# The norm's y on 128 partitions and two half pieces of 64

## The chip, the cores and the metric

The kernel runs on one core of one Trainium2 chip. The metric is the device time of one execution in microseconds (us). The engines are PE (TensorE, with PEld for its weight loads), DVE (VectorE), ACT (ScalarE), POOL (GpSimd) and SP (SyncE, here a queue of DMAs). Everything concerned here is float32.

## The reference, cut to what matters

The input is `x` of 4 images, 96 channels and 128 x 128 positions. A first layer makes 192 inner channels, runs a scan over four directions, and ends with a layer norm over the 192 channels of each position and a projection to 96:

```python
ym = (y0 + y1 + y2 + y3).reshape(B, D_INNER, H, W)
yn = jnp.moveaxis(ym, 1, -1)
mu = yn.mean(-1, keepdims=True)
var = yn.var(-1, keepdims=True)
yn = (yn - mu) * jax.lax.rsqrt(var + 1e-05) * ln_w + ln_b
yn = jnp.moveaxis(yn, -1, 1)
return jnp.einsum('bdhw,cd->bchw', yn, out_w) + out_b[None, :, None, None]
```

The result is added to `x`. A second layer then takes a group norm, splits the values by sign, computes an attention whose weights are convolution kernels, two further convolutions, and the output. The change concerns only the layer norm and its projection, called the norm here.

## The kernel before, in words

The scan (`ssm_scan`) leaves its sum over the four directions in the DRAM tensor `yms`, 192 channels by 16384 positions for each image. `ssm_output` is the norm of one image. It goes through 16 pieces of 1024 positions (`SN`), each of two halves of 512 (`CH`, one PSUM bank). A piece c passes these steps; three pieces are under way at once:

- `load_y` brings 192 channels as 96 partitions by 2 parts by 1024, one DMA on SP, three buffers. It is called for piece c + 1 in the fourth step of piece c.
- `squares(c, j)` squares part j on ACT.
- `sums(c, j)` multiplies y and its squares by a constant of 1/192 on PE (L960). The four products of a part go to four sets of 32 partitions of one bank: mean and mean square, for both halves. The two parts accumulate.
- `rows` copies that bank to SBUF on ACT (`st`, L972 and L974) and four small DMAs on ACT's queue turn it into 32 x 32 values (`mq`).
- `inverse`, `roots` and `back` make 1/sqrt(var + eps) on DVE and ACT; POOL's queue writes it to DRAM and `spread_out` reads it back onto 96 partitions (`r`), while SP loads `xr`, the piece of x.
- `projected(c, h)` is the projection of half h on PE (L1012), two products of 96 rows to 96 columns into one bank. Its weights `outws` have the norm's weight folded in and are centred over the 192 channels, so the mean need not be subtracted.
- `scaled(c, h)` multiplies the bank by r on DVE (L1025, or L1027 for image 0), `added` adds x on POOL, `counted` takes statistics on DVE, and SP stores the result.

Float32 products are two instructions each in the profile, so L1012 is 256 products and 512 instructions.

`co_run` alternates two generators by the costs that they yield. The norm of image 0 is emitted beside the scan, with three PSUM banks (`psl`). The norms of images 1, 2 and 3 are emitted beside other work, with two banks (`psr`): image 1 beside `direct_maps` of image 0, images 2 and 3 beside the attention. A bank is taken in turn by the first half's projection, the second half's projection and the sums. Up to the end of the scan `in_order` chains every engine's instructions in the order of emission; after it no such chain is set, and the framework orders them. In each round of six steps, with `old` = c - 2, the projection's halves stand apart:

```python
if old is not None:
    po = projected(old, 0)
...
yield 1.2
...
if old is not None:
    scaled(old, 0, po)
    po = projected(old, 1)
    ys.pop(old)
```

The second half is scaled in the third step, where `sums(c, 0)` stands too; `sums(c, 1)` is in the fourth and `rows(c)` in the fifth.

`other_weights` prepares the weights once, at the start, beside the projections of image 0. Loads of x for the statistics of images 1 and 2 go through POOL's queue then.

Of the kernel before, what the change touches and what calls it, by code (L numbers as in the profile page):

```python
# [9 lines left out]
F32 = mybir.dt.float32  # L10
BF16 = mybir.dt.bfloat16
AF = mybir.ActivationFunctionType
# [5 lines left out]
C = 96  # L18
H = W = 128
L = H * W  # L20
CH = 512
# [32 lines left out]
SN = 1024  # L54
# [17 lines left out]
def kernel(  # L72
# [26 lines left out]
    nc = tc.nc  # L99
    NB = x.shape[0]  # L100

    const = ctx.enter_context(tc.tile_pool(name="const", bufs=1))
# [51 lines left out]
    def filled(value, name, n=C, p=C):  # L154
        t = const.tile([p, n], F32, name=name, tag=name)
        nc.vector.memset(t, value)
        return t

    mean96 = filled(1.0 / C, "mean96")
    mean192 = filled(1.0 / (2 * C), "mean192", 32)  # L160
    zeros = filled(0.0, "zeros", 72)

    def clear(to):
# [61 lines left out]
    def other_weights():  # L225

        wdt = const.tile([128, 3, NK, 128], BF16, name="wdt", tag="wdt")
        wbc = const.tile([128, 3, 2, 128], BF16, name="wbc", tag="wbc")
        outws = const.tile([C, 2, C], F32, name="outws", tag="outws")
        outbs = const.tile([C, 1], F32, name="outbs", tag="outbs")
        with (
            tc.tile_pool(name="w0", bufs=1, side="right") as w0,
            tc.tile_pool(name="ps0", bufs=1, space=PSUM, side="right") as ps0,
        ):
            wf = w0.tile([RANK, NK, 2 * C], F32, name="wf")
            nc.gpsimd.dma_start(wf, dt_wT)  # L240
            outw = w0.tile([C, 2, C], F32, name="outw")
            nc.sync.dma_start(outw, out_wT)
            one = w0.tile([3, 128], BF16, name="one")
            nc.vector.memset(one, 1.0)
            nc.vector.memset(wdt, 0.0)
            nc.vector.memset(wbc, 0.0)
            yield
            flat = "p k c -> p (k c)"
            pieces = split3(w0, wf.rearrange(flat), [RANK, NK * 2 * C])
            for row, ch, g, p, n in (  # L250
                (row, *part)
                for img, *part in PARTS
                for row in ((KI * img,) if part[1] == 1 else (0, 64))
            ):
                for w in range(3):
                    yield
                    src = pieces[w].rearrange("p (k c) -> p k c", k=NK)[:, :, ch : ch + n]
                    for i in range(3):
                        at = row + w * 18 + i * RANK
                        nc.gpsimd.dma_start(wdt[at : at + RANK, g, :, p : p + n], src)  # L260
                for q in range(2):
                    at = row + 54 + q
                    nc.gpsimd.dma_start(wbc[at : at + 5 : 2, g, q, p : p + n], one[:, :n])
            for j in range(2):
                nc.vector.tensor_scalar(
                    outws[:, j], outw[:, j], lnw[:, j : j + 1], None, ALU.mult
                )
            pb = ps0.tile([C, 1], F32, name="pb")
            for j in range(2):
                nc.tensor.matmul(  # L270
                    pb, lhsT=outw[:, j], rhs=lnb[:, j : j + 1], start=(j == 0), stop=(j == 1)
                )
            nc.vector.tensor_add(outbs, pb, outb)

            mean = w0.tile([C, C], F32, name="mean")
            nc.vector.memset(mean, 1.0 / (2 * C))
            pw = ps0.tile([C, C], F32, name="pw")
            for j in range(2):
                nc.tensor.matmul(
                    pw, lhsT=mean, rhs=outws[:, j], start=(j == 0), stop=(j == 1)  # L280
                )
            nc.vector.tensor_sub(outws, outws, pw.unsqueeze(1).to_broadcast([C, 2, C]))
        yield wdt, wbc, outws, outbs

    def bank(ps):

# [2 lines left out]
    def part(ps, *shape):  # L289
        n = 1  # L290
        for d in shape[1:]:
            n *= d
        t = bank(ps)[: shape[0], :n]
        return t if len(shape) == 2 else t.rearrange("p (a b) -> p a b", b=shape[2])
# [636 lines left out]
    def ssm_output(b, yms, xnew, stats, ps, side, turned):  # L931
# [4 lines left out]

        with tc.tile_pool(name="c2", bufs=2, side=side) as p2:
            xb = x[b].rearrange("c h w -> c (h w)")
            ym = yms.rearrange("(j p) l -> p j l", j=2)
            rd = dram.tile([L], F32, name="rd")  # L940
            ys, sums_of, near, made = {}, {}, {}, {}

            def load_y(c):
                if c < NS:
                    ys[c] = p2.tile([C, 2, SN], F32, name="y", bufs=3)
                    nc.sync.dma_start(ys[c], ym[:, :, bass.ts(c, SN)])

            def squares(c, j):
                sq = p2.tile([C, SN], F32, name="sq")
                nc.scalar.activation(sq, ys[c][:, j], AF.Square)  # L950
                sums_of[c, j] = sq

            def sums(c, j):
                sq = sums_of.pop((c, j))
                if j == 0:
                    sums_of[c] = bank(ps)
                pm = sums_of[c]
                for g in range(4):
                    rhs = sq if g % 2 else ys[c][:, j]
                    nc.tensor.matmul(  # L960
                        pm[32 * g : 32 * g + 32],
                        lhsT=mean192[:, 0:32],
                        rhs=rhs[:, bass.ts(g // 2, CH)],
                        start=(j == 0),
                        stop=(j == 1),
                    )
# [39 lines left out]
                nc.gpsimd.dma_start(r, to.partition_broadcast(C))  # L1006
                near[c] = xr, r

            def projected(c, h):
                po = part(ps, C, CH)  # L1010
                for j in range(2):
                    nc.tensor.matmul(  # L1012
                        po,
                        lhsT=outws[:, j],
                        rhs=ys[c][:, j, bass.ts(h, CH)],
                        start=(j == 0),
                        stop=(j == 1),
                    )
                return po

            def scaled(c, h, po):
                r = near[c][1][:, bass.ts(h, CH)]
                if turned:
                    v = r.rearrange("p (h j t) -> p h j t", t=TN, j=TW)
                    nc.vector.tensor_mul(v, turned_view(po), v)  # L1025
                else:
                    nc.vector.tensor_mul(r, po, r)  # L1027
# [16 lines left out]
            for c in range(NS + 2):  # L1044
                new, old = c < NS, c - 2 if c >= 2 else None
                mid = c - 1 if 1 <= c <= NS else None
                if old is not None:
                    po = projected(old, 0)
                if mid is not None:
                    inverse(mid)  # L1050
                if new:
                    squares(c, 0)
                yield 1.2
                if mid is not None:
                    roots(mid)
                if old is not None:
                    scaled(old, 0, po)
                    po = projected(old, 1)
                    ys.pop(old)
                if new:  # L1060
                    squares(c, 1)
                yield 1.4
                if mid is not None:
                    back(mid)
                if old is not None:
                    added(old, 0)
                    scaled(old, 1, po)
                if new:
                    sums(c, 0)
                yield 1.4  # L1070
                if new:
                    sums(c, 1)
                if old is not None:
                    added(old, 1)
                    counted(old, 0)
                    load_y(c + 1)
                yield 1.4
                if new:
                    rows(c)
                if mid is not None:  # L1080
                    xr = near[mid][0]
                    nc.scalar.activation(xr, xr, AF.Identity, bias=outbs)
                    spread_out(mid)
                if old is not None:
                    counted(old, 1)
                yield 1.4
                if old is not None:
                    nc.sync.dma_start(xnew[:, bass.ts(old, SN)], near.pop(old)[turned])
                yield 1.4
# [1346 lines left out]
    class Image:  # L2436
# [50 lines left out]
    zb, yms = (  # L2487
        [dram.tile(shape, F32, name=f"{n}{p}", tag=f"{n}{p}", bufs=1) for p in range(npair)]
        for n, shape in (("zb", [2, 2 * C, NU, H, UW]), ("yms", [2, 2 * C, L]))
    )  # L2490
# [21 lines left out]
    with tc.tile_pool(name="wp", bufs=1, side="left") as wp:  # L2512
# [7 lines left out]
        for images, pace in (([0], 0.25), ([1], 0.75), ([2, 3], 1.35)):  # L2520
            left = projections(images, weights, stats, wp, psl)
            if images[0] == 0:
# [16 lines left out]
                wdt, wbc, outws, outbs = got  # L2539
# [148 lines left out]
```

## Time and profile before

| | |
|---|---|
| median of 3 runs | 6464.4 us (6441.7 to 6468.2) |
| the profiled execution | 6470.8 us, span 6468.9 us |
| PE busy | 5321.3 us, 82% of the span |
| DVE, ACT, POOL busy | 4711.2, 3786.8, 3238.6 us (73, 59, 50%) |
| granted PE clock, mean | 0.889 |
| projection L1012 | 512 instructions, 313.6 us busy |
| sums L960 on y, on the squares | 512 and 512 instructions, 215.8 and 164.7 us busy |
| squares L950 | 128 instructions of 1.04 us, 129.9 us |

The span runs from the first to the last instruction; the execution's own time includes what lies around it. A busy time is the union of a group's instructions, so products that lie side by side count once. Shares are averages over stages that are bound in different ways: the scan, the maps and the attention. What a waiting engine waited for is inferred from semaphores, and a wait for several is put down to the last. Line numbers are those of the kernel before.

### The profile page before, as it was taken

The page shows a single profiled execution, that of the slowest core. Times are in us where ns is not written, and L with a number is a line of the kernel's source. Part 1 is how long each engine was busy: PE and PEld are TensorE (multiplying, and loading weights), DVE is VectorE, ACT ScalarE, POOL GpSimd, SP SyncE. Part 2 cuts the span into 40 slices and gives each one's busy share as a digit, 9 for nine tenths or more (in the row PEclk, how much of TensorE's full clock was granted, in tenths as well). Part 3 has the DMA queues.
Part 4 walks back from the last instruction along what each step waited for, and adds up shares of the span by engine and source line. Part 5 has one row for each costly group of instructions (what it writes and reads, how often), then busy time and mean ns, then how long its engine had stood idle before and what let it go on. Part 6 is the DMA issues. An engine that isn't in the chain of part 4 may idle for free. (4 is left out here: it accounts for less than half of the span.)

```text
span 6468.9 us, 76257 instructions
## 1 busy us (share of the span) xinstructions
PE 5321.3 (82%) x23264; PEld 2301.3 (36%) x23264; DVE 4711.2 (73%) x7132; ACT 3786.8 (59%) x4770; POOL 3238.6 (50%) x2472
## 2 busy tenths in 40 slices
PE   6889988987888753989988588877888877989888
PEld 2333323322222111444433234345333445345553
DVE  4247778988989668988934785468874587888757
ACT  1247767776787676777632565466533665545642
POOL 1226757978889544979821344346213266022310
PEclk9999989998998665999999799888988988999989
DMA  6767777775675766675666776665766655966668
GB/s 154 176 157 193 191 202 196 218 213 163 199 198 163 214 173 215 197 217 174 199 182 185 187 220 161 164 157 155 213 195 164 178 145 155 243 174 181 191 170 219
DMA packets 891433, 1205.18 MB, mean 186 GB/s; under 512 B 228533, under 2 KB 743483, under 8 KB 878545
## 3 DMA queue, kind: packets, MB, share of 16 engines
q1 hardware_dynamic: 860496, 1145.35, 65.2%
q0 software_dynamic: 16208, 38.41, 2.2%
q10 hardware_dynamic: 14320, 16.54, 0.9%
q8 instruction: 187, 3.06, 0.2%
q14 instruction: 222, 1.81, 0.1%
HBM read 777.82 MB, written 345.62 MB: 174 GB/s over the span
## 5 line engine op out<-in xcount | busy, mean ns | idle before, releaser
L629 PE MATMUL bank<-y,wp 128*128 128x512 f32 (+3 forms) x3584 | 1320.2, 626 | 84.5 <-DMA y<-y 40.9
L862 POOL TENSOR_TENSOR y<-y,dl 128x1024 f32<-128x1024 f32 x384 | 1062.5, 2767 | 273.1 <-DVE dl L854 247.9
L829 POOL TENSOR_TENSOR dl<-dl,u 128x1024 f32<-128x1024 f32 x384 | 1015.8, 2645 | 247.1 <-ACT dA L805 129.5
L850 DVE TENSOR_TENSOR_SCAN dA<-dA,pBC 128x512 f32<-128x512 f32 x768 | 981.6, 1278 | 30.7
L1467 PE MATMUL two<-ya,wd 128*64 128x192 f32 (+3 forms) x2376 | 590.6, 422 | 201.7 <-ACT odd L1540 77.1
L629 PEld LDWEIGHTS bank<-y,wp 128*128 128x128 f32 (+3 forms) x3584 | 459.3, 169 | 755.8 <-issue 658.0
L854 DVE TENSOR_TENSOR dl<-dA,pBC 128x512 f32<-128x512 f32 x768 | 528.4, 688 | 260.0 <-PE pBC L743 187.1
L2159 PE MATMUL bank<-y,wn 128*64 128x384 f32 (+5 forms) x2408 | 665.2, 501 | 52.7 <-DMA y<-x1d 28.3
L743 PE MATMUL pBC<-xr,wbc 60*128 60x512 bf16 (+1 forms) x1536 | 458.5, 405 | 301.3 <-DVE dA L850 230.9
L1928 ACT COPY yb<-ya 64x768 f32<-64x768 f32 (+1 forms) x660 | 537.5, 814 | 202.6 <-PE two L1467 128.7
L672 ACT ACTIVATE dl<-pd,dtb 128x512 f32<-128x512 f32 x768 | 486.3, 684 | 183.2 <-PE pd L743 166.8
L1467 PE MATMUL two<-yb,wd 128*64 128x192 f32 (+3 forms) x2376 | 566.4, 407 | 4.0 <-ACT yb L1928 4.0
L833 DVE TENSOR_TENSOR pBC<-dl,pBC 128x512 f32<-128x512 f32 x768 | 527.5, 687 | 8.1 <-POOL dl L829 7.1
L2159 PEld LDWEIGHTS bank<-y,wn 128*64 128x64 f32 (+3 forms) x2408 | 306.9, 167 | 340.2 <-issue 150.9
L805 ACT ACTIVATE dA<-dl,negA 128x1024 f32<-128x1024 f32 x384 | 420.3, 1142 | 2.3
L1467 PEld LDWEIGHTS two<-ya,wd 128*64 128x64 f32 (+1 forms) x2376 | 266.9, 169 | 399.5 <-ACT odd L1540 87.8
L672 ACT ACT_TABLE_LOAD x248 | 318.2, 1283 | 94.9 <-PE pd L743 81.6
L743 PEld LDWEIGHTS <-wbc 60*128 60x128 bf16 (+1 forms) x1536 | 102.9, 96 | 749.3 <-issue 736.1
L1467 PEld LDWEIGHTS two<-yb,wd 128*64 128x64 f32 (+1 forms) x2376 | 295.1, 170 | 153.6 <-issue 41.5
L1012 PE MATMUL bank<-y,outws 96*96 96x512 f32 x512 | 313.6, 752 | 11.4 <-DVE r L1025 8.7
L1467 PE MATMUL two<-ya,wa 128*96 128x384 f32 (+1 forms) x528 | 229.9, 519 | 72.1 <-DMA ya<-vp 27.4
L1540 ACT COPY odd<-two 128x384 f32<-128x384 f32 (+5 forms) x176 | 116.0, 659 | 286.7 <-PE two L1482 177.2
(316 smaller groups left out, 9210.2 us busy)
## 6 DMA issues: line engine op xcount, KB each, us to landing
u<-zb SPq DMA_DIRECT2D x192, 1024.0 KB
yms<-y SPq DMA_DIRECT2D x96, 512.0 KB
y<-yms SPq DMA_DIRECT2D x64, 768.0 KB
xn<-xnew SPq DMA_DIRECT2D x128, 384.0 KB
ya<-vp SPq DMA_DIRECT2D x120, 336.0 KB
y<-y SPq DMA_DIRECT2D x128, 258.2 KB
zb<-z SPq DMA_DIRECT2D x64, 512.0 KB
ya<-x1p SPq DMA_DIRECT2D x90, 336.0 KB
```

The source lines that it names most:

```text
L629: nc.tensor.matmul(blocks(pz[p:e]), lhsT=ws[k][:, d, c : c + e - p], rhs=window(ys[k], at, d, n), start=(i == 0), stop=(i == len(terms) - 1),)
L672: nc.scalar.activation(dst, src, AF.Softplus, bias=bias)
L743: nc.tensor.matmul(p, lhsT=w[rows], rhs=xr[rows, at : at + CH], start=True, stop=True)
L805: nc.scalar.activation(live[m]["dA"], live[m]["dl"], AF.Exp, scale=negA[:, g % 3, k : k + 1])
L829: nc.gpsimd.tensor_mul(t, t, u_view(n))
L833: nc.vector.tensor_mul(p, live[n]["dl"][:, bass.ts(half, CH)], p)
L850: nc.vector.tensor_tensor_scan(h, h, p, init, ALU.mult, ALU.add)
L854: nc.vector.tensor_mul(live[n]["dl"][:, sl], live[n]["dA"][:, sl], live[n]["C", half])
L862: nc.gpsimd.tensor_add(v, v, t.rearrange("p (a b) -> p a b", b=W))
L1467: nc.tensor.matmul(of(to[p:e], r), lhsT=w[:, i, c : c + e - p], rhs=tiles(t[k][PAIR[i]][:, SLOT[i]], o, r), start=(k == 0), stop=False,)
L1928: nc.scalar.copy(yb[k][64 * h - 64 : 64 * h, :, :n], ya[k][0:64, :, h * TN : h * TN + n])
L2159: nc.tensor.matmul(pc[p:e, :n].rearrange("p (h w) -> p h w", w=W), lhsT=w[:, c : c + e - p], rhs=v[:, :, 0:W], start=(i == 0), stop=(i == ...
```

## The change

A piece of y now lies as 128 channels by 1024 positions (`y`), and the other 64 channels as two half pieces of 512 positions (`yr`), the first on partitions 0 to 63 and the second on 64 to 127. A piece takes three DMAs on SP instead of one. The squares follow that shape: 128 x 1024 and 128 x 512. The sums take four products of 128 rows and four of 64 rows, and the constant has 128 rows. The projection of a piece is emitted whole in the first step, into two banks: two products of 128 rows, then two of 64 rows, one on either half of the partitions. The weights are stacked in the same way by four DMAs on POOL's queue at the start, the 64-row part twice. The steps of the other functions stay where they are.

```diff
-    mean192 = filled(1.0 / (2 * C), "mean192", 32)
+    mean192 = filled(1.0 / (2 * C), "mean192", 32, 128)
...
-        yield wdt, wbc, outws, outbs
+            for p, e, i, c, j in (
+                (0, C, 0, 0, 0), (C, 128, 0, 0, 1), (0, 64, 1, 32, 1), (64, 128, 1, 32, 1)
+            ):
+                nc.gpsimd.dma_start(stack[p:e, i], outws[c : c + e - p, j])
+        yield wdt, wbc, stack, outbs
...
-                    ys[c] = p2.tile([C, 2, SN], F32, name="y", bufs=3)
-                    nc.sync.dma_start(ys[c], ym[:, :, bass.ts(c, SN)])
+                    y, rest = ys[c] = [
+                        p2.tile([128, n], F32, name=m, bufs=3) for m, n in (("y", SN), ("yr", CH))
+                    ]
+                    nc.sync.dma_start(y, yms[0:128, bass.ts(c, SN)])
+                    for h in range(2):
+                        nc.sync.dma_start(
+                            rest[64 * h : 64 * h + 64], yms[128:192, bass.ts(2 * c + h, CH)]
+                        )
...
-                sq = p2.tile([C, SN], F32, name="sq")
-                nc.scalar.activation(sq, ys[c][:, j], AF.Square)
+                sq = p2.tile([128, CH if j else SN], F32, name=f"sq{j}")
+                nc.scalar.activation(sq, ys[c][j], AF.Square)
...
-                    rhs = sq if g % 2 else ys[c][:, j]
+                    rhs = sq if g % 2 else ys[c][j]
+                    p = slice(64 * (g // 2), 64 * (g // 2) + 64) if j else slice(0, 128)
                     nc.tensor.matmul(
                         pm[32 * g : 32 * g + 32],
-                        lhsT=mean192[:, 0:32],
-                        rhs=rhs[:, bass.ts(g // 2, CH)],
+                        lhsT=mean192[p],
+                        rhs=rhs[p, :] if j else rhs[:, bass.ts(g // 2, CH)],
...
-            def projected(c, h):
-                po = part(ps, C, CH)
-                for j in range(2):
+            def projected(c):
+                po = [part(ps, C, CH) for _ in range(2)]
+                y, rest = ys.pop(c)
+                for h in range(2):
                     nc.tensor.matmul(
-                        po,
-                        lhsT=outws[:, j],
-                        rhs=ys[c][:, j, bass.ts(h, CH)],
-                        start=(j == 0),
-                        stop=(j == 1),
+                        po[h], lhsT=outws[:, 0], rhs=y[:, bass.ts(h, CH)], start=True, stop=False
+                    )
+                for h in range(2):
+                    p = slice(64 * h, 64 * h + 64)
+                    nc.tensor.matmul(
+                        po[h], lhsT=outws[p, 1], rhs=rest[p], start=False, stop=True
                     )
                 return po
...
                 if old is not None:
-                    po = projected(old, 0)
+                    po = projected(old)
...
                 if old is not None:
-                    scaled(old, 0, po)
-                    po = projected(old, 1)
-                    ys.pop(old)
+                    scaled(old, 0, po[0])
...
-                    scaled(old, 1, po)
+                    scaled(old, 1, po[1])
```

More of the change, by code (lines that the diff above doesn't have):

```diff
@@ L232, in other_weights @@
         wbc = const.tile([128, 3, 2, 128], BF16, name="wbc", tag="wbc")
-        outws = const.tile([C, 2, C], F32, name="outws", tag="outws")
+        stack = const.tile([128, 2, C], F32, name="outws", tag="outws")
         outbs = const.tile([C, 1], F32, name="outbs", tag="outbs")
@@ L240, in other_weights @@
             nc.gpsimd.dma_start(wf, dt_wT)
-            outw = w0.tile([C, 2, C], F32, name="outw")
+            outw, outws = (w0.tile([C, 2, C], F32, name=n) for n in ("outw", "centred"))
             nc.sync.dma_start(outw, out_wT)
@@ L938, in ssm_output @@
             xb = x[b].rearrange("c h w -> c (h w)")
-            ym = yms.rearrange("(j p) l -> p j l", j=2)
             rd = dram.tile([L], F32, name="rd")
```

## The prediction

> **What bounds the kernel now.** I read the page's first part, then the stretches of the four norms, then who waited for whom inside each, then the timeline of single pieces. A norm handles an image in 16 pieces of 1024 positions. By the starts of the copies `st<-bank` (one per piece) the norms run at 2105 to 2370 us (image 0, beside the scan), 3245 to 3525 (image 1, beside the direct maps), 3950 to 4225 and 4815 to 5090 (images 2 and 3, beside the attention). The table of these stretches:
>
> ```profile
> core 0: us, PE busy (x) PEld busy (x) DVE busy (x) ACT busy (x) POOL busy (x), PEclk, DMA share, GB/s
> 2105.00:2370.00 265.00, 193.19 (x498) 45.49 (x497) 176.22 (x243) 171.73 (x189) 143.92 (x103) 0.67 0.72 207
> 3245.00:3525.00 280.00, 241.61 (x876) 93.36 (x873) 108.77 (x236) 84.01 (x123) 63.09 (x62) 0.90 0.70 188
> 3950.00:4225.00 275.00, 245.34 (x1256) 109.70 (x1255) 115.16 (x256) 122.81 (x164) 93.72 (x124) 0.89 0.62 164
> 4815.00:5090.00 275.00, 239.79 (x1243) 104.99 (x1240) 116.33 (x258) 123.22 (x164) 99.74 (x133) 0.88 0.65 170
> ```
>
> In norms 1 to 3 PE is busy 86 to 89% and no other engine is over 45%: PE sets the pace, so PE time saved there can be span saved. In norm 0 PE is busy 73% at a clock of 0.67, DVE 66%, ACT 65%: no engine is full, and a ring of waits sets the pace. Waits of norm 1, then of norm 0, some lines of each:
>
> ```profile
> PE bank L960 <- DVE r L1025: 20.3, 9, 4.4
> ...
> PEld bank L1012 <- ACT st L972: 8.3, 8, 2.0
> ```
>
> ```profile
> PE bank L960 <- ACT sq L950: 43.1, 14, 7.1
> ...
> ACT sq L950 <- DMA y<-yms: 11.2, 5, 7.1
> ```
>
> In norm 1 the sums' product (L960) waits for the DVE product that empties the projection's bank (L1025): there are two banks. The same line is 8.3 us (3 times) in norm 2 and 7.3 (4) in norm 3. In norm 0 PE waits for the squares.
>
> **Prices on PE.** One clean piece of norm 3 on PE's timeline (each float32 product is two instructions):
>
> ```profile
> 4892.45 0.62 PE L960 MATMUL bank<-y,mean 96*32 96x512 f32 x1
> ...
> 4894.30 3.67 PE L1012 MATMUL bank<-y,outws 96*96 96x512 f32 x8
> 4897.81 0.81 PE L1467 MATMUL two<-ya,wd 128*128 128x384 f32 x2
> ```
>
> Sums take 1.85 us (4892.45 to 4894.30), eight products in four slots: products that go to four different sets of 32 output partitions start within 0.03 us of each other. The projection takes 3.51 us (to 4897.81), eight passes of about 0.43 us one after another[...].
>
> [...] The scan's two products of 60 rows at partitions 0 and 64 start together, and a stack of four products of 32 rows does too. [...]
>
> ```profile
> 1180.72 2.03 PE L531 MATMUL bank<-z,xpw 128*32 128x512 f32 x8
> 1182.69 0.61 PE L743 MATMUL pBC<-xr,wbc 120*128 120x512 bf16 x2
> ```
>
> These are four slots of two passes side by side, two slots in 128 rows by 32 columns and two in 64 by 32: 1.97 us against 4 x 0.43 = 1.72, so two changes of mode cost 0.25, about 0.12 each. [...]
>
> **The change part by part.**
> (1) Sums: four products for the 128 channels and four of 64 rows for the two half pieces. Four slots before and after; one more change of mode: +0.12 us a piece.
> (2) Projection: two products of 128 rows (four passes) and two of 64 rows on different row halves and banks, which can lie side by side (two slots): six slots for eight, -0.86 us, and a change of mode, +0.12. With (1): **-0.62 us of PE a piece**. Over the 48 pieces of norms 1 to 3 that is -30 us if all of it reached the span; if the pair never lies side by side it is +0.24 x 48 = +12.
> (3) What of it reaches the span. In 16 of the 42 pieces whose projection is followed by sums, PE then waits for DVE's r (35.9 us in all). There PE would only wait longer: gain 0. That leaves 32. The second half's first product needs the bank that ACT's copy of the sums frees (0.59 us). Before, it comes after two products of the first half (1.71 us), now after one (0.85). In about half of the pieces the projection starts as the sums end (in the quoted one, at 4894.30), the copy ends some 0.7 us later, and 0.1 us is left. The trace shows that the order after the scan isn't the emission order (at 4009.25 a first product of the projection stands before seven of the sums): where the bank is late, the first half's 64-row product goes ahead and the pair is broken, with no gain and 0.24 lost. I take 20 of the 32 as whole and the rest even: 20 x 0.62 = **-12 us**, ends -30 and +12.
> (4) Squares: 96x1024 twice (1042 ns each, `sq<-y`) becomes 128x1024 and 128x512. The trace has ACT's copy of 128x512 at 583 ns and the softplus of that shape at 684, so about 0.6: -0.44 us x 64 = -28 us of ACT. In norms 1 to 3 ACT is under half busy and PE waits for it there only 4 us: nothing. In norm 0 PE waited for squares 14 times; but where the scan's products stand between (2305.83 to 2307.65) the second square is hidden. I take 10 x 0.44 = **-4 us**, ends 0 and -7.
> (5) Norm 0's PE saves 16 x 0.62, more at half clock. Its three banks leave no bank wait. I cost it at nothing, hidden behind the wait for squares. Both halves' projection now stands ahead of the scan's L743 products, delaying those by up to two slots, 1.7 us at half clock. DVE had 4.8 us of waits on them there: 0 to +8 us, taken as 0 since B is spread a half step ahead.
> (6) Loads: one of 768 KB becomes 512 KB and two of 128 KB: 128 more issues on SP, 0.37 us each (L946's median): 47 us of SP. On SP the loads of the maps, of ya and of xr are queued behind; PE waits for any DMA in norms 1 to 3 by 2.9 us a norm at most. A load goes out about half a piece (7 us) ahead of its use: nothing; in norm 0, where ACT waited for y 11.2 us, the first square needs 512 KB only: 0 to -5. Against it, [...] SP shows waits for unrelated DMAs (27.3 us for `mq<-st` in norm 1): 0 to +10. Taken as 0. [...]
> (7) Start: four DMAs more on POOL for the stacked weights, 0.52 us each as its other issues: 2 us of POOL, which is under a third busy in the first 320 us. They wait for DVE's centring, and the statistics' loads of x are queued behind; PE's projections are the cover. Nothing, at most +2.
>
> **The sum** is -12 - 4 = -16 us. The profiled execution took 6470.8 us (span 6468.9); it would take 6455. The median of the runs is 6464.4, 6.4 lower, so I forecast **6448 us**, which is -0.25%.
>
> **The rivals.**
> A, the whole saving arrives: the pair is whole in all 48 pieces, and the pieces where PE waited gain too because the ring turns sooner: -30 us, norm 0 by (4) and (5) -7 to -12. About -40: 6424. For it: PE at 86 to 89%, and pairs elsewhere that lie side by side. Against it: 16 waits on r, and the bank.
> B, the sums wait for the emptied bank, slower. Before, 1.71 us of the second half's products stand between the end of the first half and the sums. Now both halves end together, and the sums need the first half's bank, which takes a DVE product of 0.68 us behind whatever DVE has queued, and r's landing. Queued behind the waiting sums is all of the attention's PE work. If the 26 pieces without this wait get one of 1.71 us[...], and no pair is whole: 26 x 1.71 = 44, and 12 for (2): +56, 6520. Against it: other PE work often stands between (4014.88 on, after a projection). It turns the sign when the mean new wait exceeds the mean gain, 0.3 us a piece.
> C, the pair isn't side by side and nothing else moves: +12, less 4 of ACT: 6472. The trace's pairs speak against it.
> D, the order after the scan is planned anew, and other lines than the norm's move either way, by some 20 us that nothing here prices.
>
> **How the numbers follow.** A measurement of this kernel can tell about 0.5% (32 us) from no change: faster is under 6432, slower over 6497. Forecast and its neighbourhood 0.38, A 0.27, B 0.24, C 0.11; D widens each. Faster by over 0.5%: A and a little of the forecast, 0.30. Slower: most of B, D on C, 0.27. Within: 0.43. The range goes from A with some of D, 6395, to most of B, 6510; the likeliest case's own range is 6430 to 6466.
>
> **What the new profile would show.** Right: the two 64-row passes of L1012's successor start within 0.03 us of each other in over half of the pieces of norms 1 to 3, and a clean piece takes 4.7 us instead of 5.36. `sq` gets a group of about 0.6 us. PE's waits on r grow by less than 15 us in these norms, those on st stay under 20. Wrong: the pairs start 0.4 us or more apart (C, or the broken order), sums wait for r in most pieces (B), or the time moves in stretches with no norm (D).

## The result, and the profile after

The kernel after took 6410.94 us (median; 6393.95 to 6425.22), the kernel before beside it 6462.57 (6441.66 to 6468.81): a ratio of 0.9923, interval 0.9911 to 0.9935, some 50 us less. The forecast was 16 us less. The profiled execution took 6409.7 us (span 6407.8), against 6470.8 (6468.9): these two lie 61 us apart. One profiled execution can lie up to 18 us from the median of its kernel's runs, so stages below are read from profiles and the worth of a change from medians.

**Where the time went.** A norm ends where DVE starts to combine its statistics (`mv<-xstats`). Those four points and the span's end, in us:

| | norm 0 | norm 1 | norm 2 | norm 3 | end |
|---|---|---|---|---|---|
| before | 2370.3 | 3533.0 | 4240.0 | 5095.3 | 6468.9 |
| after | 2359.9 | 3532.6 | 4211.0 | 5032.7 | 6407.8 |
| difference | -10.4 | -0.4 | -29.0 | -62.6 | -61.1 |

The 10 us at norm 0 are gone at norm 1's end. All of the gain arises between the end of norm 1 and the end of norm 3. The table of the norms' stretches in the kernel after (columns as in the prediction; the stretches are cut to the new length of each norm):

```profile
core 0: us, PE busy (x) PEld busy (x) DVE busy (x) ACT busy (x) POOL busy (x), PEclk, DMA share, GB/s
2100.00:2350.00 250.00, 164.39 (x490) 33.80 (x491) 164.40 (x227) 158.51 (x182) 131.33 (x96) 0.76 0.71 208
3245.00:3525.00 280.00, 239.54 (x887) 87.16 (x888) 109.05 (x236) 77.61 (x124) 62.71 (x62) 0.92 0.69 187
3960.00:4205.00 245.00, 222.19 (x1228) 92.30 (x1224) 113.49 (x253) 115.13 (x162) 93.82 (x123) 0.99 0.65 179
4785.00:5030.00 245.00, 220.62 (x1232) 91.54 (x1231) 113.36 (x251) 114.36 (x161) 99.31 (x131) 0.97 0.66 188
```

The column that moved is one the prediction gave no price to: PEclk, the granted clock of PE. It was 0.89 and 0.88 in norms 2 and 3, and is 0.99 and 0.97. PE's busy share hardly changed (91 and 90%, for 89 and 87%).

PE's waits that answer to those shown before, norm 1 first and then norm 0:

```profile
PE bank L970 <- DVE r L1037: 20.7, 6, 7.9
...
PEld bank L1023 <- ACT st L982: 10.5, 11, 1.6
```

```profile
PE bank L970 <- ACT sq L959: 54.2, 15, 7.5
...
ACT sq L959 <- DMA yr<-yms: 5.1, 1, 5.1
```

The sums' wait for r in norm 1 did not grow (20.3 before). Norm 0's wait for squares grew by 11 us although the squares are shorter: what PE saved there turned into waiting, and that norm kept its length (246.6 us before, 246.3 after, first sums to last projection). The clock rose there too, from 0.67 to 0.76, and bought nothing: PE's idle time within the norm went from 58 to 83 us.

**The pair.** One piece of norm 3 on PE's timeline:

```profile
4995.53 1.88 PE L1023 MATMUL bank<-y,outws 128*96 128x512 f32 x4
4997.34 1.10 PE L1028 MATMUL bank<-yr,outws 64*96 64x512 f32 x4
4998.38 0.90 PE L1770 MATMUL two<-ident,ring 96*90 96x96 f32 x8
```

Four passes of 128 rows, then four of 64 rows in the time of two: the projection takes 2.85 us (4995.53 to 4998.38), where it took 3.51. The two 64-row passes start within 0.01 us of each other. The pair is whole in 16 pieces of norm 0, 6 of norm 1, 8 of norm 2 and 12 of norm 3: 26 of 48 in norms 1 to 3. In the others the first half's 64-row product ran before the second half's 128-row one.

**The clock.** PE's clock records show only 1.0 and 0.5, and 139 of the 140 stretches at 0.5 in each of the two kernels are whole multiples of 3.41 us. Between a norm's first sums and its last projection:

| | length | at half clock | PE work lost by it | PE idle |
|---|---|---|---|---|
| norm 2, before | 267.1 | 61.4 | 27.8 | 29.5 |
| norm 2, after | 239.2 | 6.8 | 3.4 | 20.8 |
| norm 3, before | 265.2 | 68.3 | 30.0 | 34.7 |
| norm 3, after | 238.4 | 17.1 | 8.5 | 23.3 |

The third number is half of the half-clock time in which PE was busy. These two norms got 54.7 us shorter; lost work fell by 45.9 and idle time by 20.1, so about 11 us more of PE work, counted at the full clock, lies inside them, which must be work of other lines, since the norm's own became less. The half-clock time of the two norms came in 11 spells of 11.8 us on average before, and in 7 spells of 3.4 us after: the spells became fewer and, above all, shorter.

How such a loss arises is seen best in the kernel before. Its waits from 4044 to 4058 us, in norm 2 (us, times, longest):

```profile
DVE r L1025 <- DMA r<-rd: 7.0, 1, 7.0
ACT mq L992 <- DVE mq L988: 6.2, 1, 6.2
...
PE two L1467 <- ACT odd L1540: 5.8, 1, 5.8
```

DVE waits for r to come back from DRAM. Its part of the next piece's variance (L988) is queued behind, so ACT's square root (L992) waits; ACT's `odd` of the attention is queued behind that, and PE waits for `odd`. PE's timeline there, the number in brackets being the idle time before:

```profile
4050.32 0.90 PE L1760 MATMUL two<-ident,ring 96*90 96x96 f32 x8
4057.05 0.91 PE L1467 MATMUL two<-ya,wd 128*64 128x192 f32 x4 [5.82 <-ACT odd L1540]
...
4062.48 2.02 PE L1012 MATMUL bank<-y,outws 96*96 96x512 f32 x2
```

The last line is two passes in 2.02 us; two like them took 1.10 us at 4009.25, at the full clock. The same kernel cut into the stretches ahead of the gap, after it, and later:

```profile
4030.00:4051.00 21.00, 20.40 (x84) 7.67 (x82) 4.08 (x9) 6.97 (x10) 10.93 (x16) 1.00 0.57 146
4057.00:4079.00 22.00, 21.95 (x72) 7.89 (x74) 9.71 (x19) 8.26 (x11) 6.45 (x7) 0.50 0.19 51
4079.00:4100.00 21.00, 20.96 (x120) 10.33 (x117) 9.30 (x24) 8.15 (x12) 7.71 (x13) 0.99 0.53 137
```

PE counts as busy in all three. In the second it does half the work for 22 us: a gap of 5.8 us was followed by a loss of 11. The price, half of the time at half clock, shows in the passes too: those of the sums start 0.43 us apart at 4893.33, at the full clock, and 0.85 us apart at 4064.44. Why the clock stayed low for 22 us with PE busy is not shown.

### The profile page after: what moved, and what is told of

The parts are those of the page before. It is cut to its first block, busy times and chain, and to the rows that moved or that the text cites. A ratio compares the mean times of both kernels' runs of the same rounds, so it can differ in the third digit from the quotient of the medians.

```text
span 6407.8 us, 76468 instructions
## 1 busy us (share of the span) xinstructions
PE 5253.4 (82%) x23264; PEld 2254.8 (35%) x23264; DVE 4699.9 (73%) x7132; ACT 3759.4 (59%) x4770; POOL 3238.6 (51%) x2476
## 5 line engine op out<-in xcount | busy, mean ns | idle before, releaser
L2169 PE MATMUL bank<-y,wn 128*64 128x384 f32 (+5 forms) x2408 | 680.1, 507 | 58.3 <-DMA y<-x1d 34.1
L1406 POOL TENSOR_TENSOR pl<-x 96x256 f32<-96x256 f32 (+3 forms) x396 | 275.2, 710 | 0.0
```

The costliest lines, as they stand in the source:

```text
L2169: nc.tensor.matmul(pc[p:e, :n].rearrange("p (h w) -> p h w", w=W), lhsT=w[:, c : c + e - p], rhs=v[:, :, 0:W], start=(i == 0), stop=(i == ...
```

## The experiments

**Parts of the change one by one.** Four kernels in one comparison (before: 6456.98).

The move alone, on the kernel before:

```diff
-    po = projected(old, 0)
+    po = [projected(old, h) for h in range(2)]
+    ys.pop(old)
 ...
-    po = projected(old, 1)
```

> The kernel before, its y as 96 x 2, with one edit: the projections of both halves stand together in the first step, in two banks. Four theories on the gain of about 50 us. PAIR (the two 64-row products side by side save PE time): nothing here, within 10 us of before, since no pair exists. MOVE (the second half's projection ahead of the sums is what helps): 30 to 50 us under before. LAYOUT (the loads and squares on 128 partitions, and the order that the framework makes of them after the scan): within 10 us of before, since loads and squares are as before. CLOCK (PE's idle stretches of 3 us and more are gone in norms 2 and 3, so that it stays at full clock): says nothing of the cause, but the time follows the idle stretches: where five or so of them stay in norm 2, the granted clock there stays at 0.88.

6456.49 us, ratio 0.9993 (0.9981 to 1.0006). The move by itself is worth nothing that can be measured. It keeps the low clock in norm 3:

```profile
4815.00:5090.00 275.00, 239.62 (x1245) 105.38 (x1245) 113.94 (x253) 122.13 (x164) 101.55 (x132) 0.88 0.64 169
```

The new layout with the halves projected in their old steps, so without a pair:

```diff
-def projected(c):
-    po = [part(ps, C, CH) for _ in range(2)]
+def projected(c, h):
+    po = part(ps, C, CH)
```

> The changed kernel with the projections put back: each half has its own bank, a 128-row product and then its 64-row product, first half in the first step, second half in the second step. Loads, squares, sums and weights as changed. PAIR: no gain, 0 to 15 us over before for the changes of PE's mode. MOVE: no gain. LAYOUT: 30 to 50 us under before. CLOCK: where it is fast, norms 2 and 3 show a granted clock over 0.95; where slow, about 0.88.

6434.91 us, ratio 0.9958 (0.9940 to 0.9977).

The kernel after with the four products half by half, again without a pair:

```diff
 for h in range(2):
     nc.tensor.matmul(po[h], lhsT=outws[:, 0], ...)
-for h in range(2):
     p = slice(64 * h, 64 * h + 64)
     nc.tensor.matmul(po[h], lhsT=outws[p, 1], ...)
```

> The changed kernel with the four products of a projection emitted half by half: 128-row and 64-row product of the first half, then of the second. Both halves still stand in the first step. No pair lies side by side, so PE has 0.86 us more a piece where the pair was whole (26 of 48 pieces in norms 1 to 3) and a change of mode more. PAIR: the gain is gone, within 10 us of before. MOVE: 25 to 45 us under before. LAYOUT: 25 to 45 us under before. By the direct price alone it is 26 x 1.1 = 29 us over the changed kernel at most.

6431.07 us, ratio 0.9962 (0.9949 to 0.9976). In neither is any pair side by side, and yet some 25 us are gained; the other 25 come with the pair, if the kernel after's 0.9923, from another comparison, is set beside these ratios. The group of the 64-row products in this kernel, then in the kernel after (busy us, mean ns of one, idle before):

```profile
L1027 PE MATMUL bank<-yr,outws 64*96 64x512 f32 x256 | 148.6, 662 | 0.0
```

```profile
L1028 PE MATMUL bank<-yr,outws 64*96 64x512 f32 x256 | 96.2, 637 | 0.0
```

The pair takes 52 us off the busy time of these products, norm 0's pieces included, where the norm gets no shorter by it. The 26 whole pairs of norms 1 to 3 save two slots of 0.43 us each: 22 us, which fits the measured 25. The layout's part shows in the clock of norms 2 and 3, here of the kernel half by half:

```profile
3960.00:4205.00 245.00, 228.10 (x1234) 93.56 (x1234) 113.45 (x251) 114.97 (x161) 95.84 (x124) 1.00 0.66 182
4803.00:5055.00 252.00, 232.38 (x1179) 91.71 (x1186) 112.42 (x244) 109.65 (x155) 98.12 (x130) 0.93 0.63 175
```

The kernel before with y loaded by parts, so two DMAs for one:

```diff
-nc.sync.dma_start(ys[c], ym[:, :, bass.ts(c, SN)])
+for j in range(2):
+    nc.sync.dma_start(ys[c][:, j], ym[:, j, bass.ts(c, SN)])
```

> The kernel before with one edit: the load of a piece of y is two DMAs, one for each part of 96 channels, instead of one. PE, ACT and DVE do the same work. PAIR and MOVE: within 10 us of before. LAYOUT by the loads (the first square needs only its own part): 5 to 20 us under before. If the order that the framework makes after the scan is what moves the time, this edit, which moves that order as far on PE as the change does, can come out anywhere within 30 us of before, on either side.

6445.56 us, ratio 0.9989 (0.9975 to 1.0003): 7 us less (from 16 less to 2 more), not told from nothing.

**The square, from both sides.** First the kernel after with its second square stretched back to the old length:

```diff
-nc.scalar.activation(sq, ys[c][j], AF.Square)
+nc.scalar.activation(sq.rearrange("p (a n) -> p a n", a=2),
+    ys[c][1].unsqueeze(1).to_broadcast([128, 2, CH]), AF.Square)   # j == 1
```

> The kernel after, with the second square of every piece stretched back to 128x1024 (the 512 columns are squared twice, the second copy is not used), so ACT pays about 1.04 us again instead of 0.6. Loads, sums and projection stay as in the kernel after. Theory S (the layout's gain in norms 2 and 3 comes from the shorter square, because it lets sqrt and with it r come earlier): half-clock time in norms 2 and 3 goes back over 35 us each, waits of DVE on r<-rd over 20 us, and about 20 to 26 us of the gain goes: 6430 to 6437 us. Theory L (it comes from the load of y by parts, or from the order of the work): time stays within 10 us of the kernel after, 6405 to 6420, with half-clock time below 25 us in both norms. In norm 0 both expect +0 to +5.

6430.74 us, ratio 0.9950 (0.9933 to 0.9968). The two kernels below that repeat the kernel after in the same comparison have 0.9911 and 0.9919, so the stretch costs 20 to 25 us. Some 3 us of that are pairs by estimate (4 times 0.86): 22 of 48 are whole here, for 26. The edit did what it says, by the group of the second square:

```profile
L960 ACT ACTIVATE sq<-yr 128x1024 f32<-128x1024 f32 x64 | 67.0, 1047 | 12.9 <-issue 6.2 <-DMA yr<-yms 4.9 <-DMA y<-x2d 1.6
```

But it took the time by another way than theory S said. Norms 2 and 3 kept their high clock:

```profile
3970.00:4215.00 245.00, 224.62 (x1215) 91.66 (x1214) 112.48 (x252) 119.64 (x160) 92.21 (x121) 0.98 0.65 177
4798.00:5043.00 245.00, 224.56 (x1209) 89.77 (x1208) 111.13 (x242) 119.11 (x159) 97.73 (x128) 0.97 0.66 184
```

Half-clock time is 10.2 and 13.7 us there, where theory S wanted over 35. One profile, whose stages scatter by some 10 us from kernel to kernel, does not show where the 20 us went.

Then the kernel before with the second square halved:

```diff
-nc.scalar.activation(sq, ys[c][:, j], AF.Square)
+n = CH if j else SN
+nc.scalar.activation(sq[:, 0:n], ys[c][:, j, 0:n], AF.Square)
 ...
-rhs=rhs[:, bass.ts(g // 2, CH)],
+rhs=rhs[:, bass.ts(0 if j and g == 3 else g // 2, CH)],
```

> The kernel before, with the second square of every piece cut to 96x512 (about 0.6 us for 1.04); the sums take the first half's squares of that part for the second half too, so the variance of the second half's positions is left wrong: part of the squares is left out. Loads, layout, number of products, projection as before. Theory S (ACT's shorter square is most of what the new layout brings, as stretching it back in the kernel after took about 20 us of the gain away): 6440 to 6450, about -20 us. Theory C (the square is worth nothing by itself; what stretching it back cost is part of the spread between kernels): within 8 us of the kernel before. Where it falls on S, the half-clock time of norms 2 and 3 tells whether it comes by the clock (under 35 us each, for 61 and 68) or not.

6434.82 us, ratio 0.9964 (0.9948 to 0.9980): 23 us (13 to 34) by less work for ACT alone, at the old layout. Here the clock does go along, in norm 2 more than in norm 3:

```profile
3961.00:4201.00 240.00, 217.80 (x1216) 101.17 (x1214) 110.28 (x251) 114.81 (x162) 94.33 (x123) 0.96 0.70 185
4793.00:5050.00 257.00, 227.79 (x1205) 100.60 (x1204) 110.36 (x242) 113.63 (x161) 97.44 (x128) 0.91 0.67 176
```

Half-clock time 20.5 and 47.8 us, for 61.4 and 68.3. So the shorter square is worth some 20 us whether it is put in or taken out, and theory C, that it is worth nothing, has fallen. How it brings them differs between the two kernels. And the square did not change alone: in their profiles 102 and 116 of the 4770 places in ACT's order hold another instruction than in the unedited kernels. The split load changed 185 such places for 7 us, which speaks against the order as the cause, but does not exclude it.

**Six kernels that missed their aim.** They were to make r come earlier or later in norms 1 to 3. Their edits take `turned` for true in image 0; it is true in images 1 to 3. So against what the texts on record say **they reached image 0 alone**. On PE, DVE and ACT the order of instructions stayed that of the unedited kernel.

```diff
+                if mid is not None and not turned:      # one step earlier (or later)
+                    spread_out(mid)
...
-                    spread_out(mid)
+                    if turned:
+                        spread_out(mid)
```

> The kernel before with one edit: for images 1 to 3 the read-back of r from DRAM is emitted one step (1.4 us of yielded cost) earlier, with the second part's sums instead of with the copy of the sums. No engine does less work. Clock theory (long waits of PE on the chain of r cost twice, once idle and once at half clock after it): the waits of DVE on r<-rd fall from 24-30 us a norm to under 15, gaps of PE over 3 us fall from 5 to 0-2 a norm, half-clock time in norms 2 and 3 from 61 and 68 us to under 30 each, and the time falls by 25 to 50 us: 6415 to 6440. Rival (the gain of the change is PE's shorter passes and the half clock only goes along with them): waits move to other lines and the time stays within 10 us of the kernel before. Third possibility (POOL's queue then holds its additions behind r's wait for the DRAM write): slower by 10 to 30 us.

> The kernel after with the same edit: r read back one step earlier for images 1 to 3. Clock theory: few long gaps are left in norms 2 and 3 (7 and 17 us of half clock), but norm 1 still has 44 us at half clock and five gaps over 3 us; it gains up to 20 us there if something else does not hold norm 1: 6390 to 6410. Rival: no change within 10 us. POOL held behind the wait: slower by 10 to 30 us.

> The kernel after with the opposite edit: for images 1 to 3 r is read back one step later, after the copy of the sums. No engine does more work. Clock theory: DVE's waits on r<-rd rise from 10-12 us a norm to over 20, gaps over 3 us come back in norms 2 and 3 (3 or more each) and with them 35 us or more at half clock in each, and the time rises by 25 to 50 us: 6435 to 6460. Rival (the half clock is not tied to r's lateness, the gain is the shorter passes): the time stays within 10 us of the kernel after.

The early read gave 0.9992 (0.9977 to 1.0007) on the kernel before and 0.9911 (0.9889 to 0.9932) on the kernel after; the late one on the kernel after gave 0.9919 (0.9898 to 0.9941). None differs measurably from its unedited kernel. They decide nothing on the clock theory.

```diff
-nc.gpsimd.dma_start(r, to.partition_broadcast(C))
+(nc.gpsimd if turned else nc.sync).dma_start(r, to.partition_broadcast(C))
```

> The kernel before with r read back on SP's queue instead of POOL's for images 1 to 3; the order on PE, DVE and ACT is unchanged. On POOL the read stands behind additions and waits, 7 to 9 us after the write's issue, which lands after 3 to 4. Clock theory: r lands up to 3 us earlier where POOL held it, DVE's waits on r fall under 18 us a norm, half-clock time in norms 2 and 3 from 61 and 68 us to under 40, time -15 to -40. Rival 1 (the wait is not POOL's doing, the chain in front of the write is late): within 10 us. Rival 2 (SP's loads of ya, the maps and xr stand behind the wait for the write): slower by 10 to 40 us.

> The kernel after with the same edit, as a candidate that may beat it: norm 1 still has 44 us at half clock and DVE waits for r of 11 to 18 us a norm. If r comes earlier without holding SP: -5 to -20 us, 6390 to 6405. If SP is held: +10 to +40. Else within 8 us.

1.0012 (1.0000 to 1.0023) and 0.9934 (0.9917 to 0.9950): reading image 0's r on SP's queue brings nothing. No kernel tried is measurably better than the kernel after.

For norms 1 to 3 these kernels, and the next one, are repeats. Half-clock time in norms 2 and 3 together was 130, 126 and 89 us in the kernel before and its two repeats, and 24, 34, 44, 48 and 38 in the kernel after and its four. It scatters, but the two groups do not meet: the difference in clock belongs to the kernels, not to one execution.

```diff
+rd2 = rd if turned else dram.tile([L], F32, name="rd2")
 ...
 nc.gpsimd.dma_start(to.rearrange("(p f) -> p f", f=TN), q)
+if not turned:
+    again = rd2[bass.ts(c, SN)]
+    nc.gpsimd.dma_start(again, to)
+    to = again
```

> The kernel after with r's way lengthened for images 1 to 3: POOL copies each piece's 1024 values from one DRAM tensor to another before r is read back, one more DMA of 4 KB, some 4 us from issue to landing as rd's own, POOL waiting for the first to land. The order of all work on PE, DVE and ACT is that of the kernel after, so only the lateness of r changes. Clock theory (each long gap of PE is paid again at half clock): DVE's waits on r<-rd rise from 11 to 18 us a norm to over 30, gaps of PE over 3 us from 0-1 to 4 or more in norms 2 and 3, half-clock time there from 7 and 17 us to over 40 each, and the time rises by 40 to 90 us, of which a third or more is half clock. Rival (r has slack, or PE has other work to put there): within 12 us of the kernel after.

6440.57 us, ratio 0.9968 (0.9954 to 0.9981), 30 us more than the kernel after. By the profile all of it is norm 0: 279.6 us long for 246.3, while norms 2 and 3 took 241.6 and 242.0. Waits in norm 0, and one of them in the kernel after:

```profile
DVE xstats L1056 <- POOL xr L1052: 87.7, 23, 7.1
POOL rd L1009 <- DVE mq L1007: 71.9, 15, 8.2
...
POOL rd L1012 <- DMA rd<-mq: 53.7, 15, 6.3
```

```profile
DVE xstats L1051 <- POOL xr L1047: 27.7, 18, 1.8
```

POOL stands 3.6 us a piece until the first write has landed, so its additions come later, and DVE's statistics wait for these three times as long. Norm 0 gets 2.1 us a piece longer, which reaches the end. So norm 0 is sensitive to a hold on POOL's queue, found by accident: one link of the ring that the prediction spoke of. That the way of r sets norm 0's pace without the added copy is not shown: to read r earlier, later or on SP's queue in this same norm brought nothing. Nor did the shorter square and the pair, which both act there.

**All kernels side by side.** Half-clock time and PE's idle time are those of norms 2 and 3 together; the last column is the time from the end of norm 1 to the end of norm 3. All in us, from one profile each.

| kernel | ratio | half clock | idle | norm 1 to 3 |
|---|---|---|---|---|
| before | 1 | 129.7 | 64.2 | 1562 |
| before, image 0's r early; on SP | 0.9992; 1.0012 | 126.3; 88.7 | 66.6; 59.7 | 1558; 1541 |
| move alone | 0.9993 | 105.8 | 61.7 | 1545 |
| loads alone | 0.9989 | 109.3 | 36.1 | 1542 |
| short square alone | 0.9964 | 68.3 | 50.3 | 1519 |
| layout, halves apart | 0.9958 | 17.0 | 32.8 | 1512 |
| layout, half by half | 0.9962 | 34.1 | 36.4 | 1523 |
| after, long square | 0.9950 | 23.9 | 40.8 | 1507 |
| after | 0.9923 | 23.9 | 44.1 | 1500 |
| after, image 0's r early; late | 0.9911; 0.9919 | 34.1; 44.4 | 44.8; 48.9 | 1500; 1513 |
| after, image 0's r on SP; with the hop | 0.9934; 0.9968 | 47.7; 37.6 | 47.7; 44.3 | 1519; 1497 |

The last column follows the half-clock column from group to group: the kernel before and its two repeats have 115 us at half clock and 1554 us in the last column on average, the kernel after and its four have 38 and 1506. These 48 us match the measured 50. Every kernel with y on 128 partitions has little half clock. What ended PE's gaps of over 2 us in norms 2 and 3 tells which waits vanish. The sums' wait for r stays: 12.6 us on average over four kernels with y on 96 partitions (before, the move, and the two with only image 0's r changed), 14.9 over the five that keep the layout and order of after. The waits of the attention's products (`two`) for ACT's `odd` and `kt` and for DVE's `sm` fall from 32.7 us to 8.1. Between these two groups, the idle time that went was the attention's, not the norm's own.

But fewer waits alone do not bring the clock. With the loads alone split, these waits of the attention are 11.1 us and PE's idle time is 36.1, about as low as after, and yet there are 109.3 us at half clock and no gain that can be told. What sets the layouts apart is how long a spell lasts. After gaps of 2 to 3 us in norms 1 to 3, half clock followed about as often in the six kernels with y on 96 partitions (20 of 36 gaps) as in the eight with y on 128 (32 of 64), but in the median it lasted 10.0 us in the first and 3.8 us in the second.

**What stays open** is why. After the scan the framework orders the instructions anew for every kernel. To hold that order fixed while the layout changes was not tried. So whether the attention's waits went because ACT and DVE come to them sooner, or because their place in the queues changed, is not settled. Nor is it known what ends a half-clock spell, and so why spells are shorter with y on 128 partitions.

## Why the prediction was right or wrong

The forecast's range held the result and its likeliest case did not: it said 16 us, and the measured 50 lie outside its own range of 6430 to 6466. The better case, faster by over 0.5%, had 0.30. That the range held it is in part luck: its low end was put together from A and some of D, and the worth of the shorter square and the granted clock, which the runs point to, are in neither.

- **(1) and (2), prices on PE: right.** The projection takes 2.85 us, and 3.51 - 0.86 + 0.12 is 2.77; the sums with their mode change take 1.98 (3982.02 to 3984.00, norm 2) for 1.85 + 0.12. The starts side by side that these prices rest on measure, in the kernel before, under 0.01 us apart for the scan's two products of 60 rows (2200.24) and within 0.02 us for a stack of four of 32 rows (4326.02 to 4326.04).
- **(3), what reaches the span: mis-sized.** The reading of the bank and of the broken order was right in that a 64-row product ran ahead (in 22 of 48 pieces; that the bank was late in each of them was not shown), and 20 whole pairs were close to 26. But it charged the extra changes of mode, 0.12 us each by its estimate, to the span, and took the gain in the pieces with a wait as 0. Kernels that have these changes of mode and no pair are 25 us faster than before, not slower; the pair adds about 25, near the 22 that 26 whole ones bring at their full 0.86. The step took 12 us for what measured about 25.
- **(4), squares: the failed step.** Its duration was right (619 ns for "about 0.6") and so was the total (ACT's busy time 3786.8 to 3759.4, -27). Its worth was not: 4 us, and "in norms 1 to 3 ACT is under half busy and PE waits for it there only 4 us: nothing". Put in or taken out, it is worth some 20 us. PE waited little for the squares themselves; it waited for `odd` and `kt`, which stand in ACT's one queue with them, by 31.7 us in norms 2 and 3 of the kernel before. That this is the way of the 20 us is argued, not shown: with the long square put back the clock stayed high. And norm 0, where the 4 us were booked, gained nothing.
- **(5) norm 0 and (7) the start: right** within the scatter of single profiles, no gain and no loss. PE's saving went into a longer wait for the squares, as the step said.
- **(6), loads: right within the measurement**, 0.9989 for the split alone.
- **What no step priced is the granted clock.** PEclk of 0.89 and 0.88 stood in the very lines that the prediction quoted, and it read them as a busy PE. Of that busy time, 58 us in norms 2 and 3 were lost to the half clock.
- **The rivals.** B fell: the sums' waits for r were 20.7, 9.8 and 9.0 us in norms 1 to 3, against 20.3, 8.3 and 7.3. C fell, the pair lies side by side. A came nearest in size (40 us) but not by its mechanism: 22 of the 48 pairs are broken, norm 0 gave nothing, and half of the gain needs no pair. D was named without a price; of the 61 us between the two profiles 54.7 lie in norms 2 and 3, so its sign, time moving where there is no norm, did not appear, though a new order inside them may be part of the layout's gain.

## What to carry to other kernels

Read the granted clock of a stage beside its busy share before you call an engine the bound: a PE at 88% busy and a clock of 0.88 has lost time hidden in its busy time. In norms 2 and 3 of the kernel before PE was idle for 64 us and lost 58 more to the half clock, so the waits may cost about twice what the list of waits says. A saving on an engine that is far from full is not free of worth (here some 20 us came with 28 us less work for ACT), so look at who is queued behind it before costing it at nothing. And test that an edit reaches the images it names: a condition read the wrong way round cost six of these runs their question.

## What the hardware showed that was not expected

**Gaps and the clock.** PE's clock fell after 65 of 76 gaps of 3 to 5 us, and after half of those of 2 to 3 us. Over the norms 1 to 3 of the 14 profiles here, the gaps of PE that began at the full clock, by length, and how many had a half-clock spell beginning in the gap or within 1 us after it:

| gap, us | gaps | followed by half clock | its median length after the gap, us |
|---|---|---|---|
| 0.5 to 1.5 | 294 | 7 | 3.2 to 3.9 |
| 1.5 to 2 | 57 | 13 | 4.2 |
| 2 to 3 | 100 | 52 | 6.1 |
| 3 to 5 | 76 | 65 | 5.7 to 6.6 |
| over 5 | 41 | 41 | 8.7 |

Spells lasted up to 23.9 us in norms 1 to 3 of the kernel before; in the 22 us of one that are shown above, PE was busy all through. The profile models the ends of products, so the length of a single gap is not exact.

**Two row halves in one bank.** The projection's pair writes two banks. The sums' 64-row products share one: two of the four read partitions 0 to 63 and two read 64 to 127, and each of the four writes its own 32 partitions of it. They run side by side too. One piece of norm 2 in the kernel after:

```profile
4056.71 0.61 PE L970 MATMUL bank<-yr,mean 64*32 64x512 f32 x1
4056.72 0.61 PE L970 MATMUL bank<-sq,mean 64*32 64x512 f32 x1
4056.73 0.61 PE L970 MATMUL bank<-yr,mean 64*32 64x512 f32 x1
4056.73 0.61 PE L970 MATMUL bank<-sq,mean 64*32 64x512 f32 x1
...
4057.71 1.10 PE L1028 MATMUL bank<-yr,outws 64*96 64x512 f32 x2
```

The eight passes take 1.00 us (4056.71 to 4057.71), near two slots of 0.43 and the 0.12 estimated for a change of mode. In 36 of the 64 pieces all four products start within 0.02 us of each other. So in this kernel two row halves that wrote different partitions of one bank ran side by side.
